# Layer 1's last stage: expert outputs read back on GpSimd's queue, added one block later and stored one more block after that

## The chip, the cores and the metric

The kernel runs on one core of one Trainium2 chip. The metric is the device time of one launch in microseconds (us). The time before is 1188.58 us, the median of three runs (1186.8 to 1188.58).

A core has five engines, each with an instruction queue of its own, worked off in order: PE (matrix multiply), DVE (vector work), ACT (activations, copies), POOL (GpSimd) and SP (SyncE, which only issues transfers). An instruction that waits holds back everything behind it on its queue. The 16 DMA engines move the data; SP, ACT and POOL issue transfers to them. When a transfer has landed it raises a semaphore, and others wait on that.

## The reference

Two layers run on 3327 nodes with 256 features (padded to 3328 = 26 tiles of 128 nodes). Each layer is a graph convolution and then a mixture of experts: eight experts, every token goes to the two with the highest scores. The part that matters here is the end of layer 1:

```
xn = layernorm(x)
logits = xn @ router_w.T ; two best experts per token, weights renormalised
for e in range(8):
    h = gelu(xn @ w1[e] + b1[e])
    y = h @ w2[e] + b2[e]
    out = out + combine[:, e:e+1] * y        # out starts as xn
x = x + out                                   # the kernel's output
```

All of it is float32.

## The kernel before, in words

Only the tokens that an expert was chosen for are computed. Layer 1's experts work in blocks: a block is 256 token rows of one expert (a pair) or 128 rows (a single). There are 32 blocks, numbered 0 to 31 here: 26 pairs (0 to 25), then 6 singles (26 to 31). In the code `len(layer1.started)`, called `at`, is the number of blocks written out so far, so `at == 18` stands after block 17.

For each block SP loads the token rows from the list in device memory (`ring<-xlist`, L1136), w1 (L1143) and, for the later blocks, the bias b1 (L1150). PE turns the rows (L1172), multiplies by w1 (L1226), ACT applies gelu (L1234), PE multiplies by w2 (L1323). DVE adds the bias (L1330) and multiplies by the routing weight (L1331), and POOL scatters the result, 128 rows at a time, into the table `ys1` in device memory with an indirect DMA (L793, `ys<-pad,index`): two scatters for a pair, one for a single. A row of `ys1` belongs to one token and one of its two choices.

The outputs come back from `ys1` while later blocks still run. `load_outputs` (L1404) reads two tiles of 128 tokens, both choices, in one transfer of 512 KB (L1405, `ring<-ys`). `add_loaded` (L1416) adds both choices to `x` on DVE, two instructions of L1419. `store_added` (L1766) writes the finished tiles to the output from ACT's queue (L1769, 256 KB). All this stands in the loop at L1771 to L1791, once per block. Reads 1 to 7 (tiles 0 to 13) are written in the loop after `at` 18 to 24, and reads 8 to 11 (tiles 14 to 21) after `at` 27 to 30. What the loop has not added is added after it (L1799 to L1803), together with the last four tiles, which are read one at a time (256 KB, L1797) once all scatters have landed.

Dependencies: the table `ys1` is tracked as one tensor. A scatter written after a read does not wait for that read (L1255). A read waits for the scatters that stand before it in the program. The framework decides the final place of each instruction on its queue; the places and waits named below are those of the built programs.

The lines that the change touches are L1404, L1405, L1774, L1779 and L1786.

Of the kernel before, what the change touches and what calls it, by code (L numbers as in the profile page):

```python
# [64 lines left out]
FIXED = (4, 6)  # L65
# [62 lines left out]
def gnn_moe_two_layers(  # L128
# [24 lines left out]
    nc = tc.nc  # L153
# [27 lines left out]
    for name, n in BLK.items():  # L181
        at = sum(BLK[q] * (1 if q == "xT_arms" else 2) for q in blk_at)
        blk_at[name], blk_places[name] = 0, [at + i * n for i in range(1 if name == "xT_arms" else 2)]

    def blk(name, n):

        at = blk_places[name][blk_at[name] % len(blk_places[name])]
        blk_at[name] += 1
        return pad[:, at : at + n]
# [99 lines left out]
    def follow(later, earlier):  # L289
        for o in earlier:  # L290
            tc.add_manual_dep(later.ins, o.ins.name, after, reason="same rows of DRAM")

    def behind(instructions):

        if instructions and any(i is instructions[-1].ins for i in nc.cur_bb.bb.instructions):
            return tc.issue_after(instructions[-1].ins)
        return nullcontext()
# [31 lines left out]
    def statistics(t0, n, kept=None):  # L329


        mv, guess = kept or (
            work.tile([P, n, 2], F32, name="ln_mv"), work.tile([P, n], I32, name="ln_guess")
        )
        for g in range(n):
            st = work.tile([P, 6], F32, name="ln_st")
            nc.vector.bn_stats(out=st, in_=x[:, t0 + g, :])
            nc.vector.bn_aggr(out=mv[:, g, :], in_=st)
        ve = work.tile([P, n], F32, name="ln_ve")
        nc.vector.tensor_scalar(ve, mv[:, :, 1], EPS, None, ALU.add)  # L340
        nw = work.tile([P, n], F32, name="ln_nw")
        half = nw.bitcast(I32)
        nc.vector.tensor_scalar(half, ve.bitcast(I32), 1, None, ALU.logical_shift_right)
        nc.vector.tensor_scalar(guess, half, -1.0, float(0x5F3759DF), ALU.mult, ALU.add)
        rs = guess.bitcast(F32)
        for _ in range(3):
            nc.vector.scalar_tensor_tensor(nw, rs, -0.5, rs, ALU.mult, ALU.mult)  # L347
            nc.vector.tensor_tensor(nw, nw, ve, ALU.mult)
            nc.vector.scalar_tensor_tensor(rs, nw, 1.5, rs, ALU.add, ALU.mult)
        return mv, rs  # L350
# [301 lines left out]
    def rows_of(a, t0, n):  # L652
        return a[t0 * P : (t0 + n) * P, :].rearrange("(n p) d -> p n d", p=P)
# [747 lines left out]
            turn_first=turn_first, prepare_next=prepare_next, tiers_done=tiers_done(), always=always,  # L1401
        )

    def load_outputs(yt, ys, t0, n, written, group=None):  # L1404
        d = nc.sync.dma_start(  # L1405
            out=yt,
            in_=ys[t0 * P * K : (t0 + n) * P * K, :].rearrange(
                "(n p k) d -> p n (k d)", p=P, k=K
            ),
        )  # L1410
        follow(d, written)
        if group:
            tc.add_to_no_dep_group(group, d.ins)
        output_loads.append(d)

    def add_loaded(yt, t0, n):  # L1416
        x_t = x[:, t0 : t0 + n, :]
        for k in range(K):
            nc.vector.tensor_tensor(x_t, x_t, yt[:, :, k * D : (k + 1) * D], ALU.add)  # L1419
# [10 lines left out]
    ys1 = dram.tile([YROWS, D], F32, name="ys1")  # L1430
# [132 lines left out]
    written = list(outputs)  # L1563
    layer0.steps_to(late, layer0.always - 5)
    in_s = s.rearrange("p n d -> p (n d)")
    at = BEGUN * K * D
# [15 lines left out]
    for t, n in FOURS:  # L1582
        if t < BEGUN:
            yt = in_s[:, t * K * D : (t + n) * K * D]
            begun.append((yt.rearrange("p (n d) -> p n d", n=n), t, n))

    def add_begun():
        for b in begun:
            add_loaded(*b)
# [45 lines left out]
    def between():  # L1635

        load_gate(gates[1])
        normal.clear()
        second.clear()
        waiting = []  # L1640
        for pair in turned_pairs():
            waiting.append(pair)
            if len(waiting) > 1:
                second_features(*waiting.pop(0))
        second_features(*waiting.pop(0))
        outputs.clear()
        rows_written.clear()

        piece_at.clear()
        piece_at.update(AT1)  # L1650
        expect(LOADS[1])
        for pan in range(ahead):
            n_loads = len(begun) + (NCHUNK if pan == 0 else 0)
            load_pieces(NCHUNK, filter_behind, output_loads[0:n_loads])
# [22 lines left out]
    def new_layer1():  # L1677
        return experts(
            xlist1, ys1, "1", FIXED[1], D, AF.Gelu, f1_w1, f1_b1, f1_w2, f1_b2,
            nc.scalar.copy, BLOCKS1, kept=(EARLY // 2, w2_all, gate, f1_b1_sb),  # L1680
        )
# [15 lines left out]
    def panels1(layer1, turn=False):  # L1697


        def after(pan):  # L1700
            if pan < NPAN - 1:
                after1(layer1, pan)
                if turn and pan == NPAN - 2:
                    layer1.turn_first()
            else:
                list_waiting()

        return after
# [23 lines left out]
    with tc.If(first_usual > 0) as arms:  # L1732
        output_loads.clear()
        for yt, t, n in begun:
            load_outputs(yt, ys0, t, n, written, "read0")
        layer0.step(late)
        layer0.step(late)
        layer0.prepare_next()
        with behind(last_y):
            add_begun()  # L1740
        layer0.step(late)
        with behind(last_y):
            statistics(0, BEGUN, begun_stats)
        layer0.steps_to(late, layer0.always)
        between()
        layer1 = new_layer1()
        aggregate(gnn_b_sb, filter_chunk, panels1(layer1, True))
        late1 = first_blocks(layer1)

        layer1.steps_to(late1, EARLY - 1)
        layer1.step(late1, place=blk("xT_arms", DC * SB))
        baset, nbt = late1[4], late1[6]
        second_usual = usual(
            [(FIRST_TILES, baset[:, E : 2 * E]), (MORE_TILES, baset[:, 2 * E :])],
            [(late1[5][0:1, :], FIXED[1])],
            nbt[:, E : 2 * E],
        )  # L1760
        before_inner = layer1.state()
        with tc.If(second_usual > 0) as inner:  # L1762
            layer1.know(2 * E)
            waiting, asked, added, k = [], [], [], 0

            def store_added(until):  # L1766
                while added and added[0][1] <= until:
                    t, n = added.pop(0)[0]
                    nc.scalar.dma_start(out=rows_of(out, t, n), in_=x[:, t : t + n, :])  # L1769

            while len(layer1.started) < layer1.always:  # L1771
                layer1.step(late1)
                at = len(layer1.started)
                store_added(at - 2)  # L1774
                if at == EARLY + 2 * E - 2:
                    layer1.know_rest(late1)

                with behind(last_y):
                    if asked and asked[0][2] + 1 < at <= layer1.always - FIXED[1]:  # L1779
                        yt, tiles, _ = asked.pop(0)  # L1780
                        add_loaded(yt, *tiles)
                        added.append((tiles, at))
                if waiting and at > waiting[0][1] + (1 if k < FIRST_TILES // 2 else 2):
                    tiles, _, written = waiting.pop(0)
                    yt = ring[k % RING][:, PIECE - 2 * K * D :].rearrange("p (n d) -> p n d", n=2)
                    load_outputs(yt, ys1, *tiles, written, "read1")  # L1786
                    asked.append((yt, tiles, at))
                    k += 1
                if at in (EARLY + E, EARLY + 2 * E):
                    tiles = range(0, FIRST_TILES, 2) if at == EARLY + E else range(FIRST_TILES, MORE_TILES, 2)  # L1790
                    waiting.extend(((t, 2), at, list(outputs)) for t in tiles)  # L1791
            assert not waiting
            store_added(at)
            left = []
            for i, t in enumerate(range(MORE_TILES, NT)):
                yt = ring[i][:, 0 : K * D].rearrange("p (n d) -> p n d", n=1)
                load_outputs(yt, ys1, t, 1, outputs)  # L1797
                left.append((yt, (t, 1)))
            with behind(last_y):  # L1799
                for i, (yt, tiles) in enumerate([(yt, tiles) for yt, tiles, _ in asked] + left):  # L1800
                    add_loaded(yt, *tiles)
                    queue = nc.sync if i > len(asked) and i % 2 else nc.scalar
                    queue.dma_start(out=rows_of(out, *tiles), in_=x[:, tiles[0] : sum(tiles), :])  # L1803
        with inner.Else():
            layer1.back_to(before_inner)
            layer1.rest(late1)
            finish(FOURS)
    with arms.Else():
# [9 lines left out]
        layer1 = new_layer1()  # L1818
# [157 lines left out]
```

## Time and profile before

| | us |
|---|---|
| median of three runs | 1188.58 |
| the profiled execution's own time | 1192.74 |
| its span, first to last instruction | 1191.0 |
| last pair block's (25) first scatter issued | 1155.12 |
| last scatter (block 31) issued | 1172.95 |
| last add of L1419 begins | 1185.83 |

The span lies 1.74 us under the profiled execution's time, and the median of the runs 4.16 us under it. In the profile, start times are us from the span's start; "issue to landing" runs from the start of the issuing instruction to the last semaphore update of the transfer. Issuing instructions on SP and ACT carry a `q`. In a timeline, what stands in brackets is the engine's idle time just before the instruction and what ended it.

### The profile page before, as it was taken

How to read it: one execution, taken by the hardware profiler on the slowest of the kernel's cores; microseconds unless marked ns; L12 is line 12 of the kernel's file. 1: busy time of each engine (PE TensorE's matmuls, PEld its weight loads, DVE VectorE, ACT ScalarE, POOL GpSimd, SP SyncE). 2: the span in 40 equal slices, each digit the busy share in tenths (PEclk: the TensorE clock that was granted, in tenths of full speed). 3: DMA queues.
4: the chain of work that ended last, by engine and by line, in shares of the span. 5: the costliest groups of instructions: out<-in, count | busy, mean ns of one | idle time of the engine just before them, and what ended most of it. 6: DMA issues, size and time to landing. Idle time of an engine off the chain costs nothing. (4 is left out here: it accounts for less than half of the span.)

```text
span 1191.0 us, 19704 instructions
## 1 busy us (share of the span) xinstructions
PE 1152.0 (97%) x6217; PEld 1005.4 (84%) x6217; DVE 867.1 (73%) x3001; ACT 557.0 (47%) x1051; POOL 290.5 (24%) x367
## 2 busy tenths in 40 slices
PE   8999999999899999999999999999999999999973
PEld 7888888888788888888888888888888888888852
DVE  6698999988885555454545669289999998785454
ACT  5599647540233333434333346985455562043321
POOL 2111332242331112111111010022232232265531
PEclk9999999999999999999999999999999999999996
DMA  9896738724376555757565955145354451479696
GB/s 349 180 265 260 241 127 239 257 88 152 125 260 224 195 186 187 270 182 258 199 219 168 386 208 201 65 183 180 144 204 166 161 200 55 134 229 273 202 288 207
DMA packets 123185, 241.68 MB, mean 203 GB/s; under 512 B 24480, under 2 KB 93120, under 8 KB 116160
## 3 DMA queue, kind: packets, MB, share of 16 engines
q1 hardware_dynamic: 108656, 205.59, 52.7%
q0 software_dynamic: 11136, 31.60, 7.2%
q10 hardware_dynamic: 3280, 3.15, 0.8%
q8 instruction: 51, 0.84, 0.3%
q14 instruction: 62, 0.51, 0.1%
HBM read 203.98 MB, written 36.33 MB: 202 GB/s over the span
## 5 line engine op out<-in xcount | busy, mean ns | idle before, releaser
L440 PE MATMUL ps_g<-s,ring 128*128 128x256 f32 x1352 | 294.2, 380 | 0.0
L440 PEld LDWEIGHTS ps_g<-s,ring 128*128 128x128 f32 x1352 | 256.0, 190 | 34.4
L1234 ACT ACTIVATE pad<-ps_h,ring 128x256 f32<-128x256 f32 (+1 forms) x282 | 128.9, 458 | 287.2 <-PE ps_h L1226 156.1
L1226 PE MATMUL ps_h<-pad,ring 128*128 128x256 f32 (+1 forms) x1184 | 254.4, 367 | 4.4 <-ACT pad L1176 4.1
L1226 PEld LDWEIGHTS ps_h<-pad,ring 128*128 128x128 f32 x1184 | 200.9, 190 | 46.7 <-ACT pad L1234 11.1
L662 DVE SCALAR_TENSOR_TENSOR rt_product<-xn,gate 128x256 f32<-128x256 f32 x400 | 194.9, 487 | 16.1 <-ACT xn L360 2.8
L793 POOL DMA_INDIRECT ys<-pad,index x114 | 115.7, 1015 | 363.8 <-DVE pad L1281 236.1
L793 POOL DMA_INDIRECT xlist<-xn,rt_idx x104 | 115.0, 1106 | 156.9 <-DVE ln_nw L347 60.9
L1495 ACT ACTIVATE sign<-ring,below 128x416 bf16<-128x416 f32 x208 | 133.4, 641 | 13.8 <-DMA ring<-in_adjT 7.8
L470 PE MATMUL ps_g<-ring,pad 128*128 128x256 f32 x520 | 115.1, 380 | 0.8 <-DMA ring<-in_adjT 0.8
L470 PEld LDWEIGHTS ps_g<-ring,pad 128*128 128x128 f32 x520 | 98.4, 190 | 14.4 <-DMA ring<-in_adjT 1.2
L1660 ACT ACTIVATE ring<-ring 128x3328 f32<-128x3328 f32 x22 | 65.4, 2979 | 87.3 <-DVE ring L1659 56.2
L1281 DVE SCALAR_TENSOR_TENSOR pad<-ps_y,ring,pad 128x128 f32<-128x128 f32 x176 | 59.3, 348 | 47.5 <-PE ps_y L1274 47.3
L470 PE MATMUL ps_g<-ring,s 128*128 128x256 f32 x390 | 89.6, 379 | 0.0
L470 PEld LDWEIGHTS ps_g<-ring,s 128*128 128x128 f32 x390 | 74.1, 190 | 10.1
L480 DVE TENSOR_TENSOR ring<-ring,ring 128x768 f32<-128x768 f32 (+1 forms) x80 | 79.7, 1014 | 0.0
L495 PE MATMUL ps_g<-ring,s 128*128 128x256 f32 x312 | 70.2, 386 | 4.4 <-ACT s L360 4.4
L495 PEld LDWEIGHTS ps_g<-ring,s 128*128 128x128 f32 x312 | 60.1, 194 | 13.5 <-ACT s L360 5.2
L1661 ACT ACTIVATE ring<-ring 128x3328 f32<-128x3328 f32 x22 | 65.4, 2979 | 0.6
L1265 DVE TENSOR_TENSOR xnT<-pad 128x512 f32<-128x512 f32 x22 | 15.2, 692 | 59.2 <-ACT pad L1234 59.2
L1323 PE MATMUL ps_y<-ring,pad 128*128 128x256 f32 x224 | 53.8, 386 | 0.0
L776 POOL COPY xn<-rt_w 128x4 f32<-128x4 f32 x26 | 4.8, 198 | 197.8 <-DVE rt_w L738 197.8
(240 smaller groups left out, 1584.3 us busy)
## 6 DMA issues: line engine op xcount, KB each, us to landing
ring<-in_adjT SPq DMA_DIRECT2D x50, 1664.0 KB, 8.2
ring<-in_f_w1T SPq DMA_DIRECT2D x30, 1024.0 KB, 5.7
ring<-in_f_w2T SPq DMA_DIRECT2D x30, 1024.0 KB, 8.0
ring<-xlist SPq DMA_DIRECT2D x52, 258.0 KB, 3.5
ring<-in_f_w SPq DMA_DIRECT2D x36, 256.0 KB, 3.8
ring<-ys SPq DMA_DIRECT2D x12, 512.0 KB, 4.2
ring<-in_f_b SPq DMA_DIRECT2D x34, 128.0 KB, 7.6
xlist<-h2T SPq DMA_DIRECT2D x16, 257.0 KB, 7.8
```

The lines of the kernel that those rows point to most:

```text
L440: nc.tensor.matmul(ps[it], lhsT=chunks[k][:, c, ts(it, P)], rhs=s[:, j, :], start=(j == 0), stop=(j == NT - 1),)
L470: nc.tensor.matmul(ps, lhsT=b[:, c, :], rhs=a[:, c, :], start=(first and c == 0), stop=(c == CJ - 1), skip_group_check=not first,)
L480: nc.vector.tensor_tensor(out[:, part, :], out[:, part, :], other[:, part, :], ALU.add)
L495: nc.tensor.matmul(sums[pan][c], lhsT=s[:, j, ts(c, P)], rhs=piece(pan, j // CJ)[:, j % CJ, :], start=(j == 0), stop=(j == NT - 1),)
L662: nc.vector.scalar_tensor_tensor(product, xn, 1.0, gate[:, e, :], ALU.mult, ALU.mult, accum_out=sc[:, g, e : e + 1],)
L793: d = nc.gpsimd.indirect_dma_start(out=a[:, :], out_offset=bass.IndirectOffsetOnAxis(ap=index, axis=0), in_=rows_, in_offset=None,)
L1226: last_product[:] = [nc.tensor.matmul(ps, lhsT=w1[:, c, ts(hc, P)], rhs=xT[:, c, :], start=(c == 0), stop=(c == DC - 1),)]
L1234: nc.scalar.activation(hT[:, hc, :], ps, func, bias=bb1[:, hc : hc + 1])
L1281: last_y[:] = [nc.vector.scalar_tensor_tensor(part, ps, xb[:, g, WT : WT + 1], part, ALU.mult, ALU.add)]
L1495: nc.scalar.activation(sign, piece(pan, k)[:, :, ts(i, GROUP)], AF.Sign, bias=below, accum_out=positive[:, pan, i, k : k + 1],)
L1660: nc.scalar.activation(a, a, AF.Square)
L1661: nc.scalar.activation(a, a, AF.Tanh)
```

## The change

`load_outputs` takes the queue that issues the transfer. The eleven 512 KB reads of the loop are issued by POOL instead of SP; the four 256 KB reads after the loop stay on SP. A tile pair is added three iterations of the loop after its read was written, not two, and stored three iterations after its add, not two.

```
-    def load_outputs(yt, ys, t0, n, written, group=None):
-        d = nc.sync.dma_start(
+    def load_outputs(yt, ys, t0, n, written, group=None, queue=nc.sync):
+        d = queue.dma_start(
...
                 layer1.step(late1)
                 at = len(layer1.started)
-                store_added(at - 2)
+                store_added(at - 3)
...
-                    if asked and asked[0][2] + 1 < at <= layer1.always - FIXED[1]:
+                    if asked and asked[0][2] + 2 < at <= layer1.always - FIXED[1]:
                         yt, tiles, _ = asked.pop(0)
                         add_loaded(yt, *tiles)
                         added.append((tiles, at))
...
-                    load_outputs(yt, ys1, *tiles, written, "read1")
+                    load_outputs(yt, ys1, *tiles, written, "read1", nc.gpsimd)
```

In the built program, POOL's queue in this stage now reads as follows (17a is the first scatter of block 17, R1 the first read; in square brackets the scatter that a read waits for):

```
17a 17b R1[17b] 18a 18b R2[18b] 19a 19b 20a R3[19b] 20b 21a R4[20b] 21b 22a R5[21b]
22b 23a R6[22b] 23b 24a R7[23b] 24b 25a 25b 26 R8[26] 27 28 R9[27] R10[28] 29 30 31 R11[29]
```

On SP the eleven reads are gone and the other transfers keep their order. On DVE the adds of R1 to R6 stand after the results of blocks 20 to 25; before, those of R1 to R7 stood after blocks 19 to 25. On ACT one store fewer stands in the loop, and after it eight stores, not six. PE's queue is the same.

## The prediction

> **What bounds the kernel now.** The page first: PE is busy nearly throughout, so only a stretch where it is not can give anything back. Its slices are full up to the last two.
>
> ```profile
> span 1191.0 us, 19704 instructions
> PE   8999999999899999999999999999999999999973
> DMA  9896738724376555757565955145354451479696
> ```
>
> Then the stage of the change, by windows (PE busy is the second figure, the last three are clock, DMA share, GB/s): before the first read PE is full; with the reads it is at 2.43 and 1.92 of 5.
>
> ```profile
> 1102.00:1121.00 19.00, 19.00 (x99) 15.94 (x98) 8.45 (x29) 7.45 (x15) 9.70 (x10) 1.00 0.67 201
> 1131.00:1136.00 5.00, 2.43 (x14) 1.77 (x12) 2.73 (x8) 1.06 (x2) 1.11 (x2) 1.00 1.00 301
> 1156.00:1161.00 5.00, 1.92 (x15) 1.68 (x14) 2.40 (x8) 0.84 (x3) 1.67 (x3) 1.00 0.98 310
> ```
>
> Who ended the idle time, from 1119 to 1173 us (all engines) and 1119 to 1164 (SP): DVE's adds wait for their read, SP's reads wait for a scatter's landing.
>
> ```profile
> DVE x L1419 <- DMA ring<-ys: 12.2, 6, 3.1
> ...
> SPq L1405 <- DMA ys<-pad,index: 15.6, 6, 5.1
> ```
>
> One instance in the timeline. Scatter 22b takes 0.97 us on POOL, but SP's next read, which needs it landed, goes out only 5.2 us after it. PE's w1 product then starts late behind an add, and the block period, 3.91 us from 1117.38 to 1129.12 (L1226's starts), becomes 6.65, 5.38, 4.06, 4.55. Over 3.91 for a pair and 2.26 for a single (1167.29 to 1169.55), blocks 22 to 29 lose 9.6 us.
>
> ```profile
> 1142.35 0.97 POOL L793 DMA_INDIRECT ys<-pad,index  x1 [0.30 <-issue]
> ...
> 1147.53 0.38 SPq L1405 DMA_DIRECT2D ring<-ys  x1
> ```
>
> Last, the chain that ended last: the last scatter's landing (4.63), the final reads, the adds.
>
> ```profile
> 1172.95 4.63 DMA ys<-pad,index
> ...
> 1179.03 6.33 DMA ring<-ys
> ```
>
> From the last scatter's issue to the span's end are 1191.0 - 1172.95 = 18.05 us. So I ask when the last scatter can be issued.
>
> **The change part by part.**
>
> *Taken off SP.* Eleven issues of 0.38 us and 15.6 us of waits. What stood behind them is loads for blocks ahead. PE waits there for a bias once (ACT's wait for the L1150 load, 1.3 us); the rest was hidden. Worth 0 to 1.3 us on PE's path.
>
> *Adds and stores later.* The seven adds (2 x 0.69 us) become six, the seventh goes behind the last block. A block more for the read to land should end most of the 12.2 us of DVE waits, 9.6 us on PE, if the reads go out when they did. DVE's tail grows by 1.4 us (five pairs of adds, 7 us). It is covered by the 12.4 us from the last scatter's issue to the last final read's landing (1172.95 to 1185.35). The stores follow the adds; one more is issued behind the loop (0.38 us on ACT), under the same cover.
>
> *Put on POOL.* The issue: a plain transfer between two scatters there stretched their spacing from 1.27 to 1.85 us; the nearest in shape (two rows per partition, L302) took 0.76. I take 0.76 and, as the third row shows, 0.30 before the next scatter.
>
> ```profile
> 685.84 0.97 POOL L793 DMA_INDIRECT ys<-pad,index  x1 [15.11 <-issue]
> 686.81 0.58 POOL L320 DMA_DIRECT2D gate<-gate  x1
> 687.69 0.99 POOL L793 DMA_INDIRECT ys<-pad,index  x1 [0.30 <-ACT pad L1234]
> ```
>
> *The wait on POOL.* This is the dear part. The read brings its wait along: R2 waits for 18b, directly ahead of it; R3 to R7 for a scatter one place further up; R8 for 26, R10 for 28. Behind the read stand the next scatters; SP's four final reads need them all. On SP the wait held back loads for blocks ahead; here it holds back the chain that ends last.
>
> The price of a wait is the time a scatter takes to land. Two rows by the DMA view (count, median from issue to landing): 1108 to 1120 us, no reads; 1121 to 1161, with reads (3.9 to 5.8).
>
> ```profile
> ys<-pad,index POOLq DMA_INDIRECT x7, 3.0
> ...
> ys<-pad,index POOLq DMA_INDIRECT x17, 4.7
> ```
>
> I take 4.7 for the waits of R2 to R7: each waited scatter goes out about 1 us behind a 512 KB read, and the same loads and stores run beside it. The scatters of before nearest to that, 0.7 to 1.4 us after a read, took 5.5 (1136.97) and 5.8 (1155.12); against that, traffic per us falls as blocks get longer. For R8 I take 3.2 (block 26's scatter at 1160.39, after which SP's read could go at 1163.68), for R10 4.5 (1166.32, beside a read). From landing to issue 0.2 (0.15 to 0.30 at POOL's other DMA waits).
>
> Now POOL's queue, each step from the one before:
> - 17b is at 1119.08 as before and lands after 2.87; R1 at 1122.15, 18a 1.06 later (0.76 + 0.30) at 1123.21, 18b at 1124.48 (1.27 apart).
> - R2 at 1124.48 + 4.7 + 0.2 = 1129.38. 19b is 1.06 + 1.27 later, R3 4.9 after that: 1136.61.
> - R4 to R7: the waited scatter follows the read by 1.06, so the period is 1.06 + 4.9 = 5.96: 1142.57, 1148.53, 1154.49, 1160.45.
> - 24b, 25a, 25b, 26 at 1161.51 to 1165.32; R8 at 1165.32 + 3.4 = 1168.72; 27, 28 at 1169.78, 1171.05; R9 goes out while R10's wait runs; R10 at 1175.75; 29, 30, 31 at 1176.81, 1178.08, 1179.35.
>
> In short, last scatter = 1143.45 + the eight landings (28.2 + 3.2 + 4.5 = 35.9) = 1179.35, which is 6.4 us after 1172.95. DVE and PE are not later: the last add in the loop is R6's, landed some 4.3 us after 1154.49 and done 1.4 later, 1160.2, and six singles at 2.26 bring block 31's result near 1174. So the 9.6 us come back as slack before POOL's queue, not as time.
>
> *The tail.* R11 waits for 29 and goes out 2.2 us behind block 31's scatter (29 is 2.54 earlier; 4.5 + 0.2), so half a MB flows beside the final reads; before, the last of these four went out 1.6 us ahead of that scatter. Hidden it costs 0; alone at the 301 GB/s of the windows row 0.52 MB takes 1.7. I take 0.5, because DVE's add order puts R11 ahead of the final tiles but its landing should still come first.
>
> Sum: 6.4 + 0.5 = +6.9 us: a profiled execution of 1192.74 + 6.9 = 1199.6, a median of 1188.58 + 6.9 = **1195.5**.
>
> **A rule beside the rows.** The scatter rows say 3.0 quiet and 4.7 beside reads. The Trainium skill, "DMA: Bandwidth & Descriptors", section "Anatomy of one DMA — SWDGE (gpsimd) path", fits a GpSimd transfer as about 2.0 us plus bytes over 436 GB/s. For 128 KB that is an estimate of 2.3 us; eight of these put the queue's end at 1161.9, 11 us before 1172.95, PE would bound, and the change would gain. This case's own rows, all above 2.8 in this stage, decide against it.
>
> **Rivals.**
>
> 1. *The scatters land fast; faster.* With the reads spread out, landings could fall to the quiet 3.0. Then the sum is 24, the last scatter 1167.45, 5.5 us earlier: 1183. With the tail's 0.5 it turns at a mean landing of 3.6; 2.4 us (0.2%, about what a measurement of this kernel tells from no change) are gained under 3.3. For it: 3.0 at 201 GB/s. Against: reads and stores are not removed, and the smallest of the 17 is 3.9.
> 2. *The waits cancel: no change.* POOL's waits take just what DVE's waits gave: a mean between 3.3 and 3.9, 1186.2 to 1191.0. For it: the lower edge of the scatters seen with reads. Against: their median.
> 3. *The queue feeds on itself; much slower.* Read and waited scatter share POOL's queue; with 5.8 for six, 4.8 and 6.0 (1170.84) for two, the sum is 45.6, the last scatter 1189.05: +16 and 0.5 to 1.7 of tail, 1205 to 1206. For it: the scatters closest behind a read are the slow ones. Against: all queues share the DMA engines, and their load falls.
> 4. *The reads need no such wait in effect* (the scatter has landed by then). Then POOL pays only 1.06 a block, it has 1.37 to spare (3.91 - 2 x 1.27), PE gets its 9.6 back: 1179. Against: SP waits 15.6 us for the same scatters today, and POOL reaches a read sooner.
>
> **How the numbers follow.** Time = 1188.58 - 29.0 + 8 x mean landing (1143.45 - 1172.95 + 0.5 = -29.0). Forecast, mean 3.9 to 5.1, 1191 to 1200.5: 0.56. Rival 3, above 5.1: 0.18. Rival 2: 0.12. Rival 1: 0.10. Rival 4: 0.04. Faster 0.14, same 0.12, slower 0.74. The range for 8 in 10 leaves out rival 4, half of rival 1 and the far part of rival 3: 1185 to 1203.
>
> **What would show it.** In the profile after: POOL's idle time before L793 and L1405 ended by "DMA ys<-pad,index"; reads about 6 us apart from R3 to R7; scatters of blocks 24 and 25 back to back at 1.27; DVE's last L1331 several us before the last scatter; SP without waits for scatters until the final reads. The prediction is wrong if the period from R3 on is under 5 us, if POOL's queue does not stand still behind a read, or if the final reads grow by more than 1 us over 12.4 us from the last scatter.

## The result and the profile after

| | before | after |
|---|---|---|
| median of six runs each, us | 1187.12 (1185.11 to 1188.58) | 1197.85 (1193.43 to 1201.85) |
| the profiled execution's own time, us | 1192.74 | 1199.16 |
| its span, us | 1191.0 | 1197.5 |
| scatter 17b issued | 1119.08 | 1115.71 |
| last scatter (block 31) issued | 1172.95 | 1179.57 |
| from 17b to the last scatter | 53.87 | 63.86 |
| from the last scatter to the span's end | 18.05 | 17.93 |

The change makes the kernel slower: the ratio is 1.0089, 95 % interval 1.0071 to 1.0107. The forecast was 1195.5 us, with 0.74 on slower.

One thing must be kept in mind with the two profiles. The profiled execution of before was 5.6 us over its median, the one of after 1.3. And 17b goes out 3.4 us later in the profile of before (1119.08) than in that of after (1115.71), ahead of anything that the change touches. So starts are not to be compared directly; lengths counted from 17b are. From 17b to the span's end the stage takes 71.92 us before (1191.0 - 1119.08) and 81.79 after (1197.5 - 1115.71), 9.9 us more, which is close to the 10.7 us between the medians (1197.85 - 1187.12).

First the page after. The hole at the end of PE's row is deeper, and DMA's last two slices are emptier (6 and 5, before 9 and 6).

```profile
span 1197.5 us, 19695 instructions
PE   8999999999899999999999999999999999999961
DMA  9895747744385566666575963353553532668765
```

Then the stage by windows of after (length, then PE, PEld, DVE, ACT and POOL busy, granted clock, DMA share, GB/s).

```profile
1131.00:1136.00 5.00, 4.52 (x23) 3.87 (x24) 2.59 (x7) 1.53 (x3) 2.02 (x3) 1.00 0.88 287
1151.00:1161.00 10.00, 4.92 (x30) 4.24 (x30) 5.51 (x16) 1.83 (x6) 3.15 (x4) 0.94 0.67 219
1171.00:1181.00 10.00, 0.69 (x4) 0.29 (x2) 3.29 (x7) 0.00 (x0) 5.35 (x6) 0.63 0.68 216
```

The PE hole has not closed, it has moved. The first window is nearly full now, but in the second PE works half the time, and in the third it has all but finished while POOL is still at work. DVE's last result (L1331) ends at 1172.54; the last scatter goes out 7.0 us later.

Who ended the idle time, in the waits of after: all engines from 1119 to 1180 us, then SP's queue from 1119 to 1164 (us in total, times, longest).

```profile
POOL ring L1405 <- DMA ys<-pad,index: 23.8, 8, 4.4
...
DVE x L1419 <- DMA ring<-ys: 12.6, 5, 3.7
```

```profile
SPq L1136 <- DVE pad L1331: 12.7, 5, 3.7
```

SP waits for no scatter any more until the final reads. POOL does: 23.8 us in eight waits, where before it had no such wait. And DVE's adds wait for their reads as long as before (12.6 us to 1180 us against 12.2 to 1173). SP's loads of token rows (L1136) now wait 12.7 us for DVE's results, and ACT's one wait for a bias load grew from 1.3 to 4.4 us. POOL's timeline of after shows one stop after the other (start, length, instruction; in brackets the idle time ahead and what ended it).

```profile
1146.50 0.75 POOL L1405 DMA_DIRECT2D ring<-ys  x1 [3.32 <-DMA ys<-pad,index]
1147.55 1.01 POOL L793 DMA_INDIRECT ys<-pad,index  x1 [0.30 <-DVE pad L1330]
1148.86 0.97 POOL L793 DMA_INDIRECT ys<-pad,index  x1 [0.30 <-issue]
1152.85 0.75 POOL L1405 DMA_DIRECT2D ring<-ys  x1 [3.02 <-DMA ys<-pad,index]
1153.90 1.09 POOL L793 DMA_INDIRECT ys<-pad,index  x1 [0.30 <-DVE pad L1330]
1155.30 0.97 POOL L793 DMA_INDIRECT ys<-pad,index  x1 [0.30 <-DVE pad L1331]
1160.66 0.75 POOL L1405 DMA_DIRECT2D ring<-ys  x1 [4.39 <-DMA ys<-pad,index]
```

22b goes out at 1147.55, 1.05 us behind read R5. 23a follows at once. Then R6 stands still until 22b has landed, 5.30 us after 22b went out; 23b, behind R6, stands still with it. Last, the chain of after from block 26's scatter to the last add: 26's landing, R8, 27's landing, R9 and R10, and the scatters behind them.

```profile
1165.69 2.54 DMA ys<-pad,index
1168.23 0.29 issue
1168.51 0.46 POOL ring L1405
...
1169.57 5.00 DMA ys<-pad,index
...
1179.57 3.66 DMA ys<-pad,index
...
1184.74 6.56 DMA ring<-ys
...
1192.86 0.42 DVE x L1419
```

### The profile page after: what moved, and what is told of

It is laid out like the page before. It is cut to its first block, busy times and chain, and to the rows that moved or that the text cites. A ratio compares the mean times of both kernels' runs of the same rounds, so it can differ in the third digit from the quotient of the medians.

```text
span 1197.5 us, 19695 instructions
## 1 busy us (share of the span) xinstructions
PE 1151.1 (96%) x6217; PEld 1004.9 (84%) x6217; DVE 867.0 (72%) x3001; ACT 556.3 (46%) x1051; POOL 300.3 (25%) x378
## 4 chain that ended last, share of the span: by engine, by line
PE 87%; DMA 4%; DVE 4%; issue 3%; ACT 1%; POOL 1%; SPq 0%; DVEq 0%; POOLq 0%; ACTq 0%
PE ps_g L440 24%; PE ps_h L1226 18%; PE ps_g L470 16%; PE ps_y L1274 10%; PE ps_y L1323 7%; PE ps_g L495 4%; PE ptb L1172 2%; PE ps_s L395 2%; PE ps_p L1623 2%; PE ps_o L506 1%; DVE rt_product L662 1%; DMA ring<-in_f_w2T 1%; DMA ring<-ys 1%; DMA ys<-pad,index 1%; DMA x<-in_x 1%
## 5 line engine op out<-in xcount | busy, mean ns | idle before, releaser
L1234 ACT ACTIVATE pad<-ps_h,ring 128x256 f32<-128x256 f32 (+1 forms) x282 | 128.5, 457 | 289.3 <-PE ps_h L1226 155.2
L1226 PE MATMUL ps_h<-pad,ring 128*128 128x256 f32 (+1 forms) x1184 | 253.9, 367 | 5.9 <-ACT pad L1176 3.9
L1226 PEld LDWEIGHTS ps_h<-pad,ring 128*128 128x128 f32 x1184 | 200.9, 190 | 47.9 <-ACT pad L1234 9.9
L793 POOL DMA_INDIRECT ys<-pad,index x114 | 116.8, 1024 | 338.6 <-DVE pad L1281 236.0
L793 POOL DMA_INDIRECT xlist<-xn,rt_idx x104 | 114.9, 1105 | 155.4 <-DVE ln_nw L347 60.7
```

What stands on the lines that cost most here:

```text
L793: d = nc.gpsimd.indirect_dma_start(out=a[:, :], out_offset=bass.IndirectOffsetOnAxis(ap=index, axis=0), in_=rows_, in_offset=None,)
L1226: last_product[:] = [nc.tensor.matmul(ps, lhsT=w1[:, c, ts(hc, P)], rhs=xT[:, c, :], start=(c == 0), stop=(c == DC - 1),)]
L1234: nc.scalar.activation(hT[:, hc, :], ps, func, bias=bb1[:, hc : hc + 1])
```

## The experiments

Three accounts were put against each other. **Theory A:** the reads bring their wait onto POOL's queue, and each waited scatter's landing holds the scatters behind the read back. **Theory B:** it is the later adds and stores that cost. **Theory C:** it is GpSimd's way of issuing plain transfers, or their sharing a queue with the scatters, that costs, wait or no wait. The ratios are against runs of the kernel before made beside them (median 1186.72 us beside the first four, 1188.13 beside the others).

| kernel | reads on | a read waits for | adds, stores | us | ratio to before |
|---|---|---|---|---|---|
| the change | POOL | all scatters ahead | later | 1197.85 | 1.0089 (1.0071 to 1.0107) |
| queue alone | POOL | all scatters ahead | as before | 1201.24 | 1.0127 (1.0108 to 1.0147) |
| later alone | SP | all scatters ahead | later | 1184.08 | 0.9980 (0.9966 to 0.9994) |
| fewer waits, POOL | POOL | blocks 0 to 15 or 0 to 23 | later | 1179.49 | 0.9938 (0.9916 to 0.9961) |
| fewer waits, SP | SP | blocks 0 to 15 or 0 to 23 | as before | 1180.41 | 0.9951 (0.9933 to 0.9969) |
| fewer waits and later, SP | SP | blocks 0 to 15 or 0 to 23 | later | 1181.33 | 0.9935 (0.9914 to 0.9956) |
| R8 to R11 freed | POOL | R1 to R7 all, the rest 0 to 23 | later | 1193.13 | 1.0037 (1.0025 to 1.0050) |
| R1 to R7 freed | POOL | R1 to R7 0 to 15, the rest all | later | 1183.76 | 0.9957 (0.9941 to 0.9972) |
| half-size reads | POOL | all scatters ahead | later | 1191.39 | 1.0028 (1.0012 to 1.0045) |

### The queue alone

The adds and stores of before, the queue of the change. Against the change:

```
-                store_added(at - 3)
+                store_added(at - 2)
...
-                    if asked and asked[0][2] + 2 < at <= layer1.always - FIXED[1]:
+                    if asked and asked[0][2] + 1 < at <= layer1.always - FIXED[1]:
```

> POOL issues the eleven reads; adds and stores stay where they were before the change. Theory A (reads on POOL hold the scatters back for one landing each): as slow as the whole change, 0.7 to 1.1% above before, last scatter within 2 us of 1179.6, eight stops of POOL before L1405. Theory B (the later adds and stores cost the time, by their work behind the last block): within 0.2% of before.

Measured: 1.0127 of before, more than the whole change and above the 0.7 to 1.1 % expected. So the queue is what costs, and theory B falls: the later adds do not cost; by the ratios they soften the loss by about 0.4 %, with intervals that just do not touch. The waits from 1119 to 1180 us show both sides.

```profile
DVE x L1419 <- DMA ring<-ys: 20.2, 7, 5.6
POOL ring L1405 <- DMA ys<-pad,index: 19.6, 8, 4.5
```

With the earlier adds DVE stands 20.2 us for late reads, in place of 12.6 in the change. How that reaches the end isn't shown: from 17b the last scatter goes out after 62.33 us here and after 63.86 in the change, and only the tail behind it is longer, 20.43 us and not 17.93, so that the stage is 1.0 us longer by the two profiles.

### The adds and stores alone

The reads back on SP; the adds and stores as in the change.

```
-                    load_outputs(yt, ys1, *tiles, written, "read1", nc.gpsimd)
+                    load_outputs(yt, ys1, *tiles, written, "read1")
```

> Reads on SP as before; adds and stores later. Theory A: DVE's wait for a read (12.2 us before) falls below 6 us, PE gets part of 9.6 us back: 0.2 to 0.7% under before. Theory B: 0.5% or more above before.

Measured: 0.9980, a gain of 2.6 us. In this profile SP still waits 16.3 us for scatters from 1119 to 1164 us, but DVE's waits for reads are all but gone, 0.4 us from 1119 to 1174.

```profile
SPq L1405 <- DMA ys<-pad,index: 16.3, 6, 4.6
```

```profile
DVE x L1419 <- DMA ring<-ys: 0.4, 1, 0.4
```

From 17b to the last scatter it takes 51.35 us, 2.5 less than before. So this half of the change does what it says, and is worth 0.2 %. That is far less than the 9.6 us of PE that the forecast put behind DVE's waits. In this profile ACT's L1234 once waits 4.7 us for a transfer, and PE 3.8 us behind it, while SP's loads still queue behind its waits.

### Fewer waits, reads on POOL

R1 to R7 read rows of blocks 0 to 15 only, and R8 to R11 rows of blocks 0 to 23; that is when they are put on the list of reads (`at in (EARLY + E, EARLY + 2 * E)`). In the change each still waits for all scatters that stand ahead of it. Here the framework is told that the later ones do not matter. Everything else is as in the change, so reads, bytes and queues stay.

```
+            t = len(started) - 1
+            for first in (EARLY + E, EARLY + 2 * E):
+                if kept and t >= first:
+                    tc.add_to_no_dep_group(f"from{first}", d.ins)
...
+        if after:
+            tc.declare_no_dep(d.ins, group=f"from{after}", reason="not rows of these blocks")
...
-                    load_outputs(yt, ys1, *tiles, written, "read1", nc.gpsimd)
+                    load_outputs(yt, ys1, *tiles, written, "read1", nc.gpsimd, after=of)
```

> The whole change, but R1 to R7 wait only for the scatters of blocks 0 to 15 and R8 to R11 for those of blocks 0 to 23 (all rows they read), so POOL stops for a landing twice, not eight times. Theory A: the last scatter comes back by the stops that are gone, 6 x 4.8 = 29 us at most and limited by PE's pace near 1163 to 1168: 0.4 to 1.0% under before. Theory C (it is GpSimd's way of issuing a read, or read and scatter sharing a queue, that delays the scatters): still 0.5% or more above before.

Measured: 0.9938, 18 us under the change with the same reads on the same queue. The helper is longer by four to six lines here, so L1405 is L1409. POOL stops for a landing once, not twice as expected. Its waits from 1110 to 1180 us and a piece of its timeline:

```profile
POOL ring L1409 <- DMA ys<-pad,index: 2.5, 1, 2.5
```

```profile
1121.86 1.00 POOL L793 DMA_INDIRECT ys<-pad,index  x1 [0.30 <-DVE pad L1334]
1122.87 1.52 POOL L1409 DMA_DIRECT2D ring<-ys  x2
1124.70 1.02 POOL L793 DMA_INDIRECT ys<-pad,index  x1 [0.30 <-issue]
```

Two reads pass between two scatters with no stop. The landings did not get shorter: in the transfers from 1121 to 1161 us (count, median from issue to landing) the scatters take 5.6 us, and 5.0 in the change.

```profile
ys<-pad,index POOLq DMA_INDIRECT x21, 5.6
```

So it is not the landing that costs but that something waits for it: theory A is shown, by taking the wait away and leaving the transfers. The reads go out earlier with it, and DVE's adds wait 1.7 us for them from 1110 to 1180 us, not 12.6 as in the change (1119 to 1180); that fits the kernel ending up under before, and not level with it.

### Fewer waits, reads on SP; and with the later adds

The same two edits of `put` and `load_outputs` on the kernel before, first with its own adds and stores, then with the later ones.

> Before, with the same fewer waits, reads on SP, adds and stores where they were. Theory A: SP no longer stops (15.6 us before) and DVE's adds find their reads landed: last scatter 1163 to 1168, 0.4 to 1.0% under before, within 0.2% of the run on POOL with fewer waits. Theory C: clearly faster than that run, by 0.5% or more.

> The kernel before with its reads on SP, with both remedies together: R1 to R7 wait only for the scatters of blocks 0 to 15 and R8 to R11 only for those of blocks 0 to 23 (as in the run with fewer waits on SP, 0.9951 of before), and the adds and stores come later (alone 0.998 of before). The result is the full one. Theory A (all that the change lost was the wait on GpSimd's queue): with the waits gone, the later adds have only the 3.6 us of VectorE's add waits of the run with fewer waits on SP left to take, of which some reach TensorE, so 0 to 3 us under that run: 1177.5 to 1180.5 us, and within 2 us of the run with the reads on GpSimd and the same fewer waits (1179.5). Theory C (GpSimd's queue costs something of its own beside the wait, by its 0.75 us of issue per read and by sharing a queue with the scatters): this run is at least 3 us, 0.25 %, under the one on GpSimd with fewer waits: 1176.5 us or less.

Measured: 0.9951 and 0.9935. The second took 1181.33 us, 0.8 above its range; before ran 1.4 us longer beside it than beside the run that the range came from. Ahead of the final reads SP still waits for two scatters in the first, 4.6 us together, where before it was six and 15.6. The three kernels with fewer waits lie within 0.16 % of each other, with intervals of about 0.2 % to either side: with most of the waits gone, neither the queue nor the later adds make a difference that these runs can tell. Theory C falls as a cause of the loss; a cost of GpSimd's issuing up to about 0.3 % stays open. The landings say the same. In the transfers from 1121 to 1161 us of these two kernels, reads on SP, the scatters take as long as with the reads on POOL:

```profile
ys<-pad,index POOLq DMA_INDIRECT x19, 5.3
```

```profile
ys<-pad,index POOLq DMA_INDIRECT x20, 5.3
```

All three beat both the kernel before and the changed one. On SP, with the later adds in both, dropping the waits takes the ratio from 0.9980 to 0.9935: what stood behind SP's waits was not hidden once DVE's waits were gone.

### Freeing only some of the reads

The edit of fewer waits on POOL, for R8 to R11 alone and for R1 to R7 alone.

```
+ after=of if of > EARLY + E else None       # R8 to R11 freed
+ after=of if of == EARLY + E else None      # R1 to R7 freed
```

> The whole change, with R8 to R11 alone freed (they wait only for scatters of blocks 0 to 23); R1 to R7 wait as in the change. The result is the full one. Theory A counts stops: two of the eight that set the last scatter go, R8's and R10's, which took 2.5 and 5.3 us in the profile of the change, 7.8 us together with the read's own 1.06 staying. VectorE's last result was ready 7.0 us before the last scatter there (1172.54 against 1179.57), so up to 7.0 us can come back before TensorE's pace binds: last scatter about 7 us earlier, time 6 to 8 us under the change, 1190 to 1192 us, 1.003 to 1.005 of before. If what counts is the general crowding of the DMA engines and not the number of stops, the freed reads crowd the last scatters and the gain is under 3 us: 1195 us or more.

> The whole change, with R1 to R7 alone freed (they wait only for scatters of blocks 0 to 15); R8 to R11 wait as in the change. The result is the full one. Theory A: six stops of the eight go, about 31 us of POOL standing still, but TensorE's pace takes the lead long before all of that comes back (the run with all reads freed is 18 us under the change). What remains over that run is R8's stop behind block 26 and R10's behind 28, at 3 to 5 us each, less what POOL has in hand against TensorE's single blocks (2.26 a block against 1.3 a scatter): 3 to 8 us over 1179.5, that is 1182.5 to 1187.5 us, 0.996 to 1.000 of before. If the stops of R1 to R7 did not matter (only the last two reach the end), it would stay near the change, 1195 us or more.

Measured: 1.0037 and 0.9957. Both are near what counting stops gives. R1 to R7's six stops carry most of the loss, the last ones the rest.

R8 to R11 freed: the ratio is as expected, the time 1.1 us above the range given, and the way it comes about is partly another. The last scatter comes 4.1 us earlier, not 7 (59.72 us from 17b), and the tail behind it is 3.1 us shorter (14.82 us), which fits that the freed reads no longer flow beside the final ones, but is not tested alone. The 7.0 us that DVE had in hand in the change were not all free: POOL's stops also make the reads late, and DVE's adds wait for these. The waits of this kernel from 1119 to 1180 us:

```profile
POOL ring L1409 <- DMA ys<-pad,index: 18.7, 6, 5.2
...
DVE x L1425 <- DMA ring<-ys: 14.0, 5, 5.8
ACT pad L1234 <- DVE pad L1334: 10.6, 2, 7.4
PEld ptb L1172 <- ACT pad L1234: 9.9, 11, 6.8
```

An add that waits 5.8 us for its read holds up DVE's results, these ACT, and ACT holds PE. In the chain that ended last of this kernel the last scatter is reached through PE's and DVE's last block; POOL's queue, its last scatters 1.28 us apart, is just level with them:

```profile
1174.43 1.17 PE ps_y L1327 x4
1175.63 0.44 DVE pad L1334
...
1177.18 2.77 DMA ys<-pad,index
```

R1 to R7 freed: 4.3 us over the kernel with all freed by the medians, 2.3 by the ratios, where 3 to 8 was expected. The one stop for a landing that the waits of POOL show there, from 1119 to 1180 us, is short. R8 stood still for 2.0 us besides, which the profile puts down to "issue"; block 26's scatter had gone out 2.95 us before it.

```profile
POOL ring L1409 <- DMA ys<-pad,index: 1.5, 1, 1.5
```

### Half-size reads

What makes the landings as long as they are? Each read is cut to its first tile; the second tile of each pair is not read back.

```
-                    load_outputs(yt, ys1, *tiles, written, "read1", nc.gpsimd)
+                    load_outputs(yt[:, 0:1, :], ys1, tiles[0], 1, written, "read1", nc.gpsimd)
```

> The whole change, with each of the eleven reads cut to its first tile, 256 KB in place of 512 KB, and everything else as in the change: the second tile of each pair is not read back, so the output is wrong for tiles 1, 3 ... 21 and the adds use stale data there. The waits and their places are the same. It asks what sets the landing of 4.8 us of a waited scatter, the mis-sized term of the forecast. If it is the bytes of the read that flows beside it, the mean landing falls to between 3.4 and 4.2 (half-way to the 3.0 without reads): eight landings 27 to 34 us in place of 38.6, 1186 to 1193 us. If it is that a transfer stands ahead of the scatter on GpSimd's own queue, whatever its size, or the loads and stores on the other queues, the landings stay at 4.5 to 5 and the time at 1195 to 1199 us, 1.007 to 1.01 of before.

Measured: 1.0028, 1191.39 us, within the range that the bytes give. From 1121 to 1161 us the scatters' median falls from 5.0 in the change to 3.8 (count, KB each for plain transfers, median); the first fence is the change, the second the half-size reads.

```profile
ring<-ys POOLq DMA_DIRECT2D x6, 512.0 KB, 4.5
...
ys<-pad,index POOLq DMA_INDIRECT x13, 5.0
```

```profile
ring<-ys POOLq DMA_DIRECT2D x6, 256.0 KB, 3.3
...
ys<-pad,index POOLq DMA_INDIRECT x15, 3.8
```

Counted from the issue of the waited scatter to that of the read, the six stops of R2 to R7 come to 32.55 us in the change and to 22.67 here. It is not a clean comparison: in this build R3 to R7 stand directly behind the scatter that they wait for, not one scatter further on, so that POOL waits longer for the same landing. In spite of this the 17b-to-last-scatter time falls from 63.86 to 58.73 us. Towards the end the order differs too: R11 goes out ahead of block 31's scatter here. So the bytes of the reads stretch the landings of the scatters. Whether it is the read just ahead or the whole traffic of the stage, which falls from 242 to 214 GB/s with it, this run does not separate, nor what keeps the 3.8 us above the quiet 3.0.

## Why the prediction was right, and which term was off

The sign, the place and the mechanism were as forecast; the medians differ by 10.7 us, not by 6.9. The absolute miss is smaller, 2.35 us, because the base was 1188.58 and came to 1187.12; that is luck.

- **The wait moves to POOL: right.** POOL's idle time before L1405 is ended by the landing of a scatter, eight times; before L793 it mostly is not, since the scatter behind a read finds its read just issued (0.30). SP has no wait for scatters left until the final reads. Reads R3 to R7 are 5.67, 6.65, 6.35 and 7.81 us apart, "about 6" at first and longer at the end. Blocks 24 and 25's scatters go out 1.30 and 1.40 us apart, not 1.27.
- **The landing: the term that was mis-sized.** "I take 4.7 for the waits of R2 to R7", that is 4.9 from the waited scatter to the read. Measured are 5.37, 4.91, 4.62, 5.59, 5.30 and 6.76, for R8 2.82 (3.4 forecast) and for R10 4.98 (4.7): 40.35 in place of 37.5 us, +2.85. Without the 0.2, R2 to R7 average 5.2, about midway between the 4.7 taken and the two rows that the working set aside, 5.5 and 5.8 for scatters 0.7 to 1.4 us behind a read. It set them aside because "traffic per us falls as blocks get longer". Traffic did fall, from 263 to 242 GB/s between 1121 and 1161 us, and the scatters' median still rose from 4.7 to 5.0, so the mean rate was the wrong guide. "About 1 us behind a 512 KB read" holds for four of the six; by the working's own steps 18b and 19b go out 2.3 us behind theirs, and they were not quicker (5.37 and 4.91).
- **R10's stop is not R10's landing.** Block 28's scatter landed in 3.9 us, less than the 4.5 taken. The forecast let R9 go out while R10's wait ran; in the chain R9 itself stands for 27, which went out at 1169.57 and landed 5.00 us later, and R10 follows R9 at once. That the sum came near here is in part luck.
- **Smaller steps on POOL's queue.** R1 waited not for 17b but for its buffer: the timeline puts the idle time down to PE's L1226, and it left 3.32 us after 17b (3.07 forecast). Scatters that followed one another were up to 0.18 us further apart than 1.27. Together +0.74. The read's 0.75 us and the 0.30 behind it came as forecast (0.76, 0.30). With the landings: 60.27 + 2.85 + 0.74 = 63.86 us from 17b to the last scatter.
- **The tail: +0.5 forecast, -0.1 measured.** The last read to land took 12.4 us from the last scatter, as before. R11 did flow beside the final reads, and the run with R8 to R11 freed had 3.1 us less tail, but before there were late reads in that place too.
- **Adds a block later: half right.** "A block more for the read to land should end most of the 12.2 us of DVE waits, 9.6 us on PE, if the reads go out when they did." Alone on SP it does end the waits, 0.4 us are left, but 2.6 us are gained and not 9.6. What the prediction called hidden behind SP's waits ("worth 0 to 1.3 us") then came to the fore: without these waits the ratio fell by another 0.45 %. In the change the reads do not go out when they did, and 12.6 us of waits remain. That the adds only make "slack before POOL's queue" was too simple: without the later adds the loss is 0.4 % larger by the ratios.
- **The rivals.** Rival 1 (landings near 3.0) and rival 2 (a mean under 3.9) would have needed landings that only the half-size reads come near. Rival 3 was the right direction for the landing, with a mean of 4.84 (40.35 / 8, less 0.2) where it had 5.7. Rival 4, no wait in effect, did not happen in the change, but its time (1179, 0.992 of its base) is close to what the kernel takes once the wait is really taken away (0.9938).
- **The rule of the page.** By the fit of the Trainium skill, "DMA: Bandwidth & Descriptors", section "Anatomy of one DMA — SWDGE (gpsimd) path", the estimate for a scatter was 2.3 us; the change's median is 5.0, and even with half-size reads it is 3.8. The measured rows decide. The same section says that DMA engines do not wait on semaphores but the issuing sequencer does, before dispatch; that agrees with the 23.8 us of POOL's waits above.

## What to carry to other kernels

A transfer takes its wait along to the queue that issues it. Before moving one to another engine's queue, ask what stands behind it there: here it was the scatters of the chain that ends last, and eight times they stood behind a read that waited for a landing, mostly of about 5 us. Look first at whether the wait is needed at all: naming the blocks whose rows a read really depends on gained 0.5 to 0.65 % over before on either queue, where later use alone gained 0.2 %, and with that done the queue made no difference that these runs can tell.

## What the runs showed of the hardware

- A scatter of 128 KB took 2.6 to 3.5 us to land in the last 8 us ahead of the first read (after). The scatters that R2 to R7 waited for, one or two places behind a 512 KB read on POOL, took 4.6 to 6.8, those behind 256 KB reads 3.0 to 4.6, both counted from the scatter's issue to that of the read. It is not the place behind a read alone: 24b, directly behind R7, landed in 3.9 us, when 135 GB/s flowed (1161 to 1171 us); and with the reads on SP and fewer waits the scatters' median was 5.3. Nor does the mean DMA rate of the stage tell it: with R1 to R7 freed it was 270 GB/s and the scatters' median 3.8, and no read went out from 1133.8 to 1158.1 us; in the change it was 242 GB/s and 5.0.
- A 512 KB read held POOL for 0.75 us, one of 256 KB for 0.57; two 512 KB reads in a row took 1.51 together, and the 0.30 ahead of the next scatter came once. The bytes do not set it: earlier in the profile of before an 8 KB load (`f_r_sb<-in_f_rT`) held POOL for 0.75 us and a load of 1024 KB (`gate<-gate`) for 0.58 to 0.64. The transfers of 0.75 bring two pieces to each partition, the shorter ones one; that is a reading of their shapes, and no run here tests it alone.

```profile
1145.48 0.57 POOL L1405 DMA_DIRECT2D ring<-ys  x1 [2.47 <-DMA ys<-pad,index]
1146.35 0.99 POOL L793 DMA_INDIRECT ys<-pad,index  x1 [0.30 <-issue]
```

These two lines are from POOL's timeline with half-size reads.
